# A selective-scan kernel: the products of two of four states moved to TensorE transposes, part of them to GpSimd, Softplus in one function, and the side work placed anew

## The chip, the cores and the metric

The kernel runs on one core of one Trainium2 chip. Its time is the device time of one execution in microseconds; "faster" and "slower" compare the medians of several executions. The core has five engines that each work through their own queue of instructions in program order: TensorE (PE), VectorE (DVE), ScalarE (ACT), GpSimd (POOL) and SyncE (SP, which here issues the DMAs). An instruction that waits for a semaphore holds everything behind it in its own queue, and nothing in another one.

## The reference

An image of 256 x 256 tokens with 128 channels goes through two layers, each of the form x + layer(group_norm(x)). Layer 0 is a gated attention along rows. Layer 1, in which the change lies, projects to 256 channels, applies a 3x3 depthwise convolution and SiLU, and then runs a selective scan over all 65,536 tokens in four directions (k = 0 to 3: along rows, along columns, and both backwards), with 16 states per channel:

```
delta = softplus(dt_w @ (x_proj_dt @ xs) + dt_b)          # per channel and token
h[t]  = exp(delta[t] * A) * h[t-1] + (delta[t] * xs[t]) * B[t]     # 16 states per channel
y[t]  = sum over the states of h[t] * C[t]  + D * xs[t]
```

B and C (16 values each) depend on the token, not on the channel. The four directions are summed, layer-normalised, multiplied by a gate and projected back to 128 channels.

## The kernel before

**Chunks, steps, slots.** The scan goes direction by direction (`ORDER = (2, 1, 3, 0)`) in chunks of T = 512 tokens: 128 chunks per direction, 512 in all, numbered q. A chunk has 8 steps, g = 0 to 7, one for each group of 32 channels. A tile of a step has 128 partitions: partition 32*j + c is channel c of the group with the states 4*j to 4*j+3, so `NI` = 4 states lie behind each other along the free dimension. A step handles them one after another; n = 0 to 3 counts them, and (g, n) names such a slot below: (5,3) is the last slot of step 5, and (0,0) comes after (7,3) in the next chunk. There are 4096 steps.

**What a slot does.** In each slot ScalarE computes one exponential `dA = exp(A * delta)` from `dr` (delta spread over the partitions by a DMA, through DRAM), into PSUM (`dA`) or, for one kind of state, into SBUF (`dAl`); then VectorE runs one `tensor_tensor_scan` with it. The other operand of the scan, B*delta*x, comes in two ways:

- For the first `NB` = 3 states of the four, VectorE multiplies `B_r` (B, spread over the partitions by a DMA) with `ur` (delta*x spread over the partitions by a TensorE matmul with `spread`, in PSUM), in one instruction per step, `times_B`, after the scan of slot 1.
- For the last state, ScalarE multiplies on tokens: `turn` transposes delta*x (`du`) so that tokens lie on the partitions (`tpd`, copied to `duT`); `products` multiplies it by B as a scalar per partition, 16 products of 128 x 128 for each half of the channels, into `bt`; `turn_back` transposes four blocks of it per step back into PSUM (`bl`), from which the scan reads. The slot with `bl` comes first in a step.

After the four slots GpSimd copies the last column of the step (`hst`) and multiplies the 128 x 2048 result by `C_r` (the C product). `sums` adds the states up with 16 matmuls by `gather` into `yp`, for four steps at a time: steps 0 to 3 in (5,3) and (6,0), steps 4 to 7 in (1,0) of the next chunk. `evacuate` copies `yp` to `yo`.

**Order by hand.** `tc.manual_schedule()` keeps each engine's queue in the order in which the program states the instructions. The main loop states a slot's exponential, then pieces of side work, then the scan, then (n = 1) the next step's `times_B`, and (n = 3) the next step's `bl` and the `ur` of the step after it. The side work is written as generators; each `yield` ends a piece, and one piece per slot is stated. Side work is: `prepare(q + 2)`, from (5,1) on: transposes `tps` of the tokens, copies to `xs`, the projection `pb` and its copy `bc`, the matmuls `pv`, softplus, `du`, and the loads of `B_r` and `C_r`; `turn(q + 1)` from (4,3) on; `products`, in numbers per slot given by the table `counts`; and, for a chunk that has been summed, `store` (its `tpy`, `yt`) or, in the last direction, `finish` (`ysum`, `ys`, statistics, `yn`, `tpz`, `gz`, `po`, `xo`), each from (3,0) of the next chunk on. Softplus is written out as relu(v) + log1p(exp(-|v|)), with Abs, Relu, Exp, two Identity and Ln on ScalarE and three operations on GpSimd.

**PSUM.** Eight banks: two for all side work (`tag="mm"`, in turn), one each for `bl`, `ur` and `yp`, three for `dA`. A tile with one buffer is written again only when its last reader is done.

The slots in which the pieces of `prepare` stand follow from the yields: in the kernel before, `pb` is stated in (7,0) and `bc` in (7,2); the copies of `turn` in (5,0) and (5,1).

Of the kernel before, what the change touches and what calls it, by code (L numbers as in the profile page):

```python
# [16 lines left out]
P = 128  # L17
# [49 lines left out]
def attention_and_scan_kernel(  # L67
# [568 lines left out]
    NI = 4  # L636
    NB = 3
    sw = ctx.enter_context(tc.tile_pool(name="sw", bufs=1))
# [36 lines left out]
    for q in range(4):  # L675
# [3 lines left out]
        )  # L679
    neg_one = sw.tile([P, 1], F32, name="neg_one")  # L680
    nc.vector.memset(neg_one, -1.0)
    hst = sw.tile([P, NG, NI], F32, name="hst")
# [38 lines left out]
    def prepare(q):  # L721
# [5 lines left out]
        for h in range(2):  # L727
# [6 lines left out]
            yield  # L734
        yield from until(2, 5)
        for h, tp in enumerate(tps):
# [3 lines left out]
        for h in range(2):  # L740
            nc.tensor.matmul(  # L741
                pb, xw_in[:, k, h, :], xs[:, h, :], start=(h == 0), stop=(h == 1)
            )
        yield
        yield
        bc = io.tile([R + 2 * NS, T], F32, name="bc", bufs=1)
# [3 lines left out]
        yield  # L750


        e = io.tile([P, 2, T], F32, name="e", bufs=1)
        delta = io.tile([P, 2, T], F32, name="delta", bufs=1)
        pvs = []
        for h in range(2):
            pv = sps.tile([P, T], F32, name="pv", tag="mm")
            nc.tensor.matmul(  # L758
                pv, dtw_s[:, k, h * P : (h + 1) * P], bc[:R, :], start=True, stop=True
            )  # L760
            pvs.append(pv)
        yield
        yield
        for h, pv in enumerate(pvs):
            nc.scalar.activation(e[:, h, :], pv, AF.Abs, bias=dtb_s[:, k, h : h + 1])  # L765
            nc.scalar.activation(delta[:, h, :], pv, AF.Relu, bias=dtb_s[:, k, h : h + 1])
            yield
        tp = sps.tile([P, 4, R + 2 * NS], F32, name="tpb", tag="mm")
        for b in range(4):
            nc.tensor.transpose(  # L770
                tp[:, b, :], bc[:, b * P : (b + 1) * P], ident[: R + 2 * NS, : R + 2 * NS]
            )
        nc.scalar.activation(e, e, AF.Exp, scale=-1.0)
        B_r = io.tile([P, NB, T], F32, name="B_r")
        C_r = io.tile([P, NI, T], F32, name="C_r")
        for m, t, ni in ((0, B_r, NB), (1, C_r, NI)):
            for j in range(4):
                n = m * NS + NI * j
                nc.sync.dma_start(
                    t[32 * j : 32 * j + 32],  # L780
                    bc_d[n : n + ni, :].unsqueeze(0).to_broadcast([32, ni, T]),
                )
        yield
        lg = io.tile([P, 2, T], F32, name="lg", bufs=1)
        nc.scalar.activation(lg, e, AF.Identity, bias=1.0)
        yield
        du = io.tile([P, 2, T], F32, name="du")
        nc.scalar.activation(du, lg, AF.Identity, bias=neg_one)
        B_t = io.tile([P, 4, R + 2 * NS], F32, name="B_t")
        nc.scalar.copy(B_t, tp)  # L790
        yield
        nc.gpsimd.tensor_tensor(e, e, du, ALU.subtract)  # L792
        yield
        yield
        nc.scalar.activation(lg, lg, AF.Ln)  # L795
        yield
        nc.gpsimd.tensor_tensor(lg, lg, e, ALU.add)  # L797
        yield
        nc.gpsimd.tensor_tensor(delta, delta, lg, ALU.add)  # L799
        de_d = sd.tile([DI, T], F32, name="de_d")  # L800
        nc.sync.dma_start(de_d.rearrange("(h p) t -> p h t", p=P), delta)
        yield
        nc.gpsimd.tensor_tensor(du, delta, xs, ALU.mult)  # L803
        prepared[q] = xs, de_d, du, B_r, C_r, B_t

    def turn(q):

        duT = io.tile([P, 4, DI], F32, name="duT", bufs=1)
        turned[q] = duT
        tps = []  # L810
        for w in range(2):
            tp = sps.tile([P, 2, DI], F32, name="tpd", tag="mm")
            for b in range(2):
                for h in range(2):
                    t0 = (2 * w + b) * P
                    nc.tensor.transpose(
                        tp[:, b, h * P : (h + 1) * P], prepared[q][2][:, h, t0 : t0 + P], ident
                    )
            tps.append(tp)
        yield  # L820
        for w, tp in enumerate(tps):
            nc.scalar.copy(duT[:, 2 * w : 2 * w + 2, :], tp)
            yield

    def products(q, h):


        bt = wk.tile([P, 4, 4, 4, 32], F32, name=f"bt{h}", bufs=1)
        products_of[q, h] = bt
        duT, B_t = turned[q], prepared[q][5]  # L830
        for b in range(4):
            for j in range(4):
                n = R + NI * j + NB
                nc.scalar.mul(  # L834
                    bt[:, b, :, j, :],
                    duT[:, b, h * P : (h + 1) * P].rearrange("t (g c) -> t g c", c=32),
                    B_t[:, b, n : n + 1],
                )
                yield

    def turn_back(q, g):

        bl = sps.tile([P, T], F32, name="bl", bufs=1)
        bt = products_of[q, g // 4]
        for b in range(4):
# [4 lines left out]

    def spread_delta(q, h):

        de_d = prepared[q][1]
        dr = io.tile([P, 4, T], F32, name="dr")
        for j in range(4):
            nc.sync.dma_start(
                dr[32 * j : 32 * j + 32],
                de_d[h * P : (h + 1) * P, :].rearrange("(q c) t -> c q t", c=32),
            )
        return dr  # L860
# [86 lines left out]
    def finish(q, yos):  # L947
# [39 lines left out]
        yn = io.tile([P, 4, DI], F32, name="yn", tag="yl", bufs=1)  # L987
        for j, now, then in ((0, 15, 16), (1, 16, 19), (2, 19, 20), (3, 20, 27)):
            nc.scalar.activation(
# [8 lines left out]
        for h in range(2):  # L998
# [5 lines left out]
            tps.append(tp)  # L1004
        yield from until(27, 31)
        gz = io.tile([P, 2, T], F32, name="gz", bufs=1)
        for h, tp in enumerate(tps):
# [88 lines left out]
    bls = {(0, 0): turn_back(0, 0)}
    multiplying.append(products(0, 1))
    for _ in range(4):
        piece(multiplying)


    counts = {1: [0, 0, 2, 2], 3: [2, 2, 2, 2], 5: [0, 0, 3, 3], 6: [2, 2, 2, 2], 7: [2, 2, 2, 0]}
    for s, (q, g) in enumerate(all_steps):
        k, a = steps[q]
        nxt = all_steps[s + 1] if s + 1 < len(all_steps) else None
        if g == 1:
            drs[q, 1] = spread_delta(q, 1)
        if g == 2 and q and steps[q - 1][0] != ORDER[0]:
            summed[q - 1] = load_sum(q - 1)
        if g == 2 and q + 2 < NQ:  # L1110
            load(q + 2)
        if g == 5 and q + 1 < NQ:
            drain(preparing)
            drs[q + 1, 0] = spread_delta(q + 1, 0)
        dr = drs[q, g // 4][:, g % 4, :]
        hs = bxs.pop((q, g))
        for n, i in enumerate((NB, *range(NB))):
            if i < NB:
                dA = sps.tile([P, T], F32, name="dA", bufs=3)
            else:  # L1120
# [27 lines left out]
            nc.vector.tensor_tensor_scan(  # L1148
                hs[:, i, :],
                dA,  # L1150
                hs[:, i, :] if i < NB else bls.pop((q, g)),
                0.0 if a == 0 else hst[:, g, i : i + 1],
# [12 lines left out]
        if g % 4 == 3:  # L1165
            del drs[q, g // 4]
        nc.gpsimd.tensor_copy(hst[:, g, :], hs[:, :, T - 1])  # L1167
        nc.gpsimd.tensor_tensor(hs, hs, prepared[q][4], ALU.mult)  # L1168
# [65 lines left out]
```

## Time and profile before

| what | value |
| --- | --- |
| median of 3 runs | 32186.01 us (32183.83 to 32190.26) |
| the profiled execution: its span, the only time that the page gives of it | 32185.1 us |
| busy, share of the span: VectorE, GpSimd, ScalarE, TensorE | 92%, 80%, 78%, 74% |
| first `hst` copy (end of step 0 of chunk 0) | at 5596.6 us |
| `hst` of step 0 of chunks 128, 256, 384 | at 12149.7, 18700.4, 25251.4 us |
| a chunk in the first three directions: (25251.4 - 5596.6) / 384 | 51.2 us, 6.4 per step |
| a chunk in the last direction, with `finish` (steps 3072 to 4088: 6.731 us each) | 53.85 us |
| q1, the queue of SP's DMAs: bytes | 3476.09 MB |

The layer 0 and the front of layer 1 take the first 5.5 ms. Everything after is the scan. The page gives, in its first two parts, the busy time of each engine and its busy share in 40 slices; `PEclk` is the clock granted to TensorE, in tenths of the full one. The groups list busy time, mean duration and the idle time of the engine ahead of the group's instructions, with what ended that idle time. Consecutive instructions of one engine overlap by some tens of nanoseconds, so a cost in a full queue is the distance from start to start, which the timeline gives.

### The profile page before, as it was taken

To read this page: it belongs to the slowest core of one execution; us is meant where nothing else is said; L and a number is where in the kernel's file an instruction comes from. 1 tells how busy PE (TensorE), PEld (TensorE's weight loads), DVE (VectorE), ACT (ScalarE), POOL (GpSimd) and SP (SyncE) were. 2 spreads that over 40 slices of the span, in tenths; PEclk is the share of its full clock that TensorE was granted. 3 is DMA by queue.
4 is the path that set the end of the run, shared out by engine and by line. 5 is a ranking of instruction groups with operands and counts; after the bars stand their busy time and mean duration, and the time that the engine had idled before them with its cause. 6 is when DMAs were issued, how large, how long until landed. Compare 5 with 4: busy or idle time off the path is not lost.

```text
span 32185.1 us, 380702 instructions
## 1 busy us (share of the span) xinstructions
PE 23853.4 (74%) x122902; PEld 10868.3 (34%) x122902; DVE 29575.2 (92%) x29023; ACT 25201.0 (78%) x50438; POOL 25710.4 (80%) x11291
## 2 busy tenths in 40 slices
PE   6999988666676667777777777777777777777777
PEld 3555544222222222222222232223222333333333
DVE  7666633999999999999999999999999999999999
ACT  5555522888888888888888888888888888888888
POOL 4222200999999999999999999999999999999998
PEclk9999999888888888888888888888888888888888
DMA  4001033444444444444444444444444555555554
GB/s 143 30 28 29 27 105 121 110 109 108 111 109 108 110 110 118 119 121 120 119 120 122 119 119 121 121 119 119 122 119 118 123 124 124 123 123 123 124 123 113
DMA packets 2100469, 3518.55 MB, mean 109 GB/s; under 512 B 201112, under 2 KB 1187096, under 8 KB 2022560
## 3 DMA queue, kind: packets, MB, share of 16 engines
q1 hardware_dynamic: 2093296, 3476.09, 43.3%
q8 instruction: 967, 15.84, 0.2%
q10 hardware_dynamic: 5168, 18.12, 0.1%
q14 instruction: 1038, 8.50, 0.1%
HBM read 2754.18 MB, written 739.25 MB: 109 GB/s over the span
## 4 chain that ended last, share of the span: by engine, by line
PE 32%; ACT 24%; DVE 22%; issue 12%; POOL 9%; DMA 2%; SPq 0%; ACTq 0%; POOLq 0%; DVEq 0%
DVE bx L1148 11%; PE yp L890 8%; DVE bx L875 7%; ACT dA L1122 6%; PE ur L864 6%; POOL bx L1168 5%; PE pb L741 3%; ACT bt L834 2%; PE pc L563 2%; ACT dAl L1122 2%; PE av L393 2%; PE tpy L913 2%; POOL at L370 2%; ACT e L765 2%; ACT L795 2%
## 5 line engine op out<-in xcount | busy, mean ns | idle before, releaser
L1168 POOL TENSOR_TENSOR bx<-bx,C_r 128x2048 f32<-128x2048 f32 x4096 | 18604.4, 4542 | 334.3 <-POOL hst L1167 5.8
L1148 DVE TENSOR_TENSOR_SCAN bx<-dA,hst,bx 128x512 f32<-128x512 f32 x12192 | 15074.4, 1264 | 217.2 <-ACT dA L1122 215.3
L1122 ACT ACTIVATE dA<-dr,A_s 128x512 f32<-128x512 f32 x12288 | 8329.3, 683 | 2247.5 <-DVE bx L1148 2199.6
L864 PE MATMUL ur<-du,spread 128*128 128x512 f32 x8192 | 5710.1, 787 | 4498.5 <-DVE bx L875 4378.8
L875 DVE TENSOR_TENSOR bx<-B_r,ur 128x1536 f32<-128x1536 f32 x4096 | 7075.5, 1727 | 40.1 <-DMA dr<-de_d 40.1
L834 ACT ACTIVATE bt<-duT,B_t 128x128 f32<-128x128 f32 x16384 | 5572.5, 392 | 698.7 <-PE bl L846 698.7
L1148 DVE TENSOR_TENSOR_SCAN bx<-dAl,hst,bl 128x512 f32<-128x512 f32 x4064 | 5096.6, 1254 | 24.2 <-PE bl L846 24.1
L890 PE MATMUL yp<-bx,gather 128*32 128x512 f32 x32768 | 5052.5, 771 | 7.5 <-POOL bx L1168 6.4
L846 PE MATMUL bl<-ident,bt 128*128 128x128 f32 x16384 | 2714.8, 289 | 2441.0 <-DVE bx L1148 2439.0
L846 PEld LDWEIGHTS bl<-ident,bt 128*128 128x128 f32 x16384 | 1791.0, 143 | 4323.4 <-DVE bx L1148 3240.7
L864 PEld LDWEIGHTS ur<-du,spread 128*128 128x128 f32 x8192 | 1451.2, 223 | 5027.9 <-DVE bx L875 5023.9
L370 POOL TENSOR_TENSOR at<-at,sm 128x2048 f32<-128x2048 f32 x256 | 922.2, 3603 | 2719.7 <-DVE sm L369 2550.6
L1122 ACT ACTIVATE dAl<-dr,A_s 128x512 f32<-128x512 f32 x4096 | 2919.2, 713 | 0.0
L890 PEld LDWEIGHTS yp<-bx,gather 128*32 128x32 f32 x32768 | 1165.1, 139 | 4348.3 <-issue 3834.9
L1167 POOL COPY hst<-bx 128x4 f32<-128x4 f32 x4096 | 771.4, 188 | 1615.5 <-DVE bx L1148 1588.6
L362 ACT ACTIVATE at<-at,mx 128x256 f32<-128x256 f32 x2048 | 1016.1, 498 | 472.5 <-DVE mx L358 468.1
L792 POOL TENSOR_TENSOR e<-e,du 128x1024 f32<-128x1024 f32 x512 | 1202.8, 2349 | 138.3 <-DMA C_r<-bc_d 138.3
L799 POOL TENSOR_TENSOR delta<-delta,lg 128x1024 f32<-128x1024 f32 x512 | 1209.9, 2363 | 40.1
L803 POOL TENSOR_TENSOR du<-delta,xs 128x1024 f32<-128x1024 f32 x512 | 1205.4, 2354 | 40.2
L758 PE MATMUL pv<-bc,dtw_s 8*128 8x512 f32 x2048 | 1019.6, 616 | 256.5 <-ACT bc L747 256.5
L797 POOL TENSOR_TENSOR lg<-lg,e 128x1024 f32<-128x1024 f32 x512 | 1205.0, 2354 | 0.2 <-ACT lg L795 0.2
L391 DVE COPY aT<-atp 128x512 f32<-128x512 f32 x512 | 353.6, 691 | 774.8 <-PE atp L382 771.0
(173 smaller groups left out, 31933.7 us busy)
## 6 DMA issues: line engine op xcount, KB each, us to landing
dr<-de_d SPq DMA_DIRECT2D x4096, 256.0 KB
C_r<-bc_d SPq DMA_DIRECT2D x2048, 256.0 KB
B_r<-bc_d SPq DMA_DIRECT2D x2048, 192.0 KB
de_d<-delta SPq DMA_DIRECT2D x512, 512.0 KB
xtok<-xc_d SPq DMA_DIRECT2D x256, 512.0 KB
xtok<-xc_d SPq DMA_DIRECT2D x512, 256.0 KB
yl<-y_d SPq DMA_DIRECT2D x512, 256.0 KB
y_d<-yt SPq DMA_DIRECT2D x512, 256.0 KB
```

The costliest lines, as they stand in the source:

```text
L370: nc.gpsimd.tensor_tensor(at, at, sm.unsqueeze(3).to_broadcast([P, H, 2, S]), ALU.mult,)
L797: nc.gpsimd.tensor_tensor(lg, lg, e, ALU.add)
L799: nc.gpsimd.tensor_tensor(delta, delta, lg, ALU.add)
L803: nc.gpsimd.tensor_tensor(du, delta, xs, ALU.mult)
L834: nc.scalar.mul(bt[:, b, :, j, :], duT[:, b, h * P : (h + 1) * P].rearrange("t (g c) -> t g c", c=32), B_t[:, b, n : n + 1],)
L846: nc.tensor.transpose(bl[:, b * P : (b + 1) * P], bt[:, b, g % 4].rearrange("t j c -> t (j c)"), ident)
L864: nc.tensor.matmul(ur, spread[:, g % 4].rearrange("p j c -> p (j c)"), prepared[q][2][:, g // 4, :], start=True, stop=True,)
L875: nc.vector.tensor_tensor(bx[:, :NB, :], prepared[q][3], ur.unsqueeze(1).to_broadcast([P, NB, T]), ALU.mult,)
L890: nc.tensor.matmul(yp[32 * g : 32 * g + 32, :], gather, hc[:, i, :], start=(i == 0 and steps[q][0] != ORDER[0]), stop=True, skip_group_che ...
L1122: nc.scalar.activation(dA, dr, AF.Exp, scale=A_s[:, k, g // 4, g % 4, i : i + 1])
L1148: nc.vector.tensor_tensor_scan(hs[:, i, :], dA, hs[:, i, :] if i < NB else bls.pop((q, g)), 0.0 if a == 0 else hst[:, g, i : i + 1], ALU.mult,
L1168: nc.gpsimd.tensor_tensor(hs, hs, prepared[q][4], ALU.mult)
```

## The change

- `NB` becomes 2: `times_B` covers two states, and two states of four take the way over tokens, with their own tiles `bt{h}{i}` and PSUM banks `bl0`, `bl1`. `dA` goes from three PSUM banks to two. The order of the states in a step is 2, 0, 3, 1, so that the slots 0 and 2 read `bl0` and `bl1`. `turn_back` is stated after slot 1 (`bl0`) and after slot 3 (`bl1`, ahead of `ur`).
- `products` makes 64 products per chunk, two in every slot (`PER = 2`); every fourth is a `tensor_scalar` on GpSimd (`SHARE = 4`), the others stay on ScalarE. They begin in (3,0) and (7,0).
- Softplus is one ScalarE function; the chain of Abs, Relu, Exp, Identity, Ln and the three GpSimd operations go, `du` stays on GpSimd.
- The pieces of `prepare`, `turn` and `finish` stand in other slots. By the yields `pb` is stated in (6,2), `bc` in (7,0), `pv` in (7,1), Softplus in (7,3), `du` in (0,2), the loads of `B_r` and `C_r` in (2,1); the transposes of `turn` in (1,3) and (2,0), its copies in (2,0) and (2,1). `finish` has 42 slots instead of 59.
- `dr` is loaded for two steps at a time instead of four, two steps ahead; `duT` has two buffers. Before the loop all products of chunk 0 and the whole of `prepare(1)` are made.

The diff, cut to its core:

```diff
-    NB = 3
+    NB = 2
+    SHARE = 4
...
 # prepare
-        yield from until(2, 5)
+        yield from until(2, 3)
...
-        yield
-        yield
+        yield from until(5, 7)
         bc = io.tile([R + 2 * NS, T], F32, name="bc", bufs=1)
         nc.scalar.copy(bc, pb)
...
+        yield from until(8, 10)
+        for h, pv in enumerate(pvs):
+            nc.scalar.activation(
+                delta[:, h, :], pv, AF.Softplus, bias=dtb_s[:, k, h : h + 1]
+            )
+        de_d = sd.tile([DI, T], F32, name="de_d")
+        nc.sync.dma_start(de_d.rearrange("(h p) t -> p h t", p=P), delta)
         yield
-        yield
-        for h, pv in enumerate(pvs):
-            nc.scalar.activation(e[:, h, :], pv, AF.Abs, bias=dtb_s[:, k, h : h + 1])
-            nc.scalar.activation(delta[:, h, :], pv, AF.Relu, bias=dtb_s[:, k, h : h + 1])
-            yield
         tp = sps.tile([P, 4, R + 2 * NS], F32, name="tpb", tag="mm")
...
-        nc.scalar.activation(e, e, AF.Exp, scale=-1.0)
+        yield from until(11, 13)
+        du = io.tile([P, 2, T], F32, name="du")
+        nc.gpsimd.tensor_tensor(du, delta, xs, ALU.mult)
+        B_t = io.tile([P, 4, R + 2 * NS], F32, name="B_t")
+        nc.scalar.copy(B_t, tp)
...
+        yield from until(13, 20)
         for m, t, ni in ((0, B_r, NB), (1, C_r, NI)):
...
-        nc.scalar.activation(lg, e, AF.Identity, bias=1.0)
-        nc.scalar.activation(du, lg, AF.Identity, bias=neg_one)
-        nc.gpsimd.tensor_tensor(e, e, du, ALU.subtract)
-        nc.scalar.activation(lg, lg, AF.Ln)
-        nc.gpsimd.tensor_tensor(lg, lg, e, ALU.add)
-        nc.gpsimd.tensor_tensor(delta, delta, lg, ALU.add)
...
 # turn
-            tps.append(tp)
+            yield
+            nc.scalar.copy(duT[:, 2 * w : 2 * w + 2, :], tp)
         yield
-        for w, tp in enumerate(tps):
-            nc.scalar.copy(duT[:, 2 * w : 2 * w + 2, :], tp)
-            yield
...
 # products
+        bts = [wk.tile([P, 4, 4, 4, 32], F32, name=f"bt{h}{i}", bufs=1) for i in range(NI - NB)]
+        for i, bt in enumerate(bts):
+            for b in range(4):
+                for j in range(4):
+                    n = R + NI * j + NB + i
+                    to = bt[:, b, :, j, :]
+                    of = duT[:, b, h * P : (h + 1) * P].rearrange("t (g c) -> t g c", c=32)
+                    by = B_t[:, b, n : n + 1]
+                    if SHARE and (4 * b + j) % SHARE == SHARE - 1:
+                        nc.gpsimd.tensor_scalar(to, of, by, None, ALU.mult)
+                    else:
+                        nc.scalar.mul(to, of, by)
+                    yield
...
 # finish
-        for j, now, then in ((0, 15, 16), (1, 16, 19), (2, 19, 20), (3, 20, 27)):
+        for j, now, then in ((0, 15, 16), (1, 16, 19), (2, 19, 20), (3, 20, 23)):
...
-        yield from until(27, 31)
+        yield from until(23, 25)
...
-        yield from until(55, 58)
+        yield from until(39, 41)
...
 # main loop
-        if g == 1:
-            drs[q, 1] = spread_delta(q, 1)
+        if g % 2 == 0 and s + 2 < len(all_steps):
+            drs[all_steps[s + 2]] = spread_delta(*all_steps[s + 2])
...
-        if g == 5 and q + 1 < NQ:
-            drain(preparing)
-            drs[q + 1, 0] = spread_delta(q + 1, 0)
...
-        for n, i in enumerate((NB, *range(NB))):
+        for n, i in enumerate((NB, 0, NB + 1, 1)):
             if i < NB:
-                dA = sps.tile([P, T], F32, name="dA", bufs=3)
+                dA = sps.tile([P, T], F32, name="dA", bufs=2)
...
-            if g == 4 and n == 3 and q + 1 < NQ:
+            if n == 3 and g == 1 and q + 1 < NQ:
                 turning.append(turn(q + 1))
-            if g == 5 and n == 2 and q + 1 < NQ:
+            if n == 0 and g == 3 and q + 1 < NQ:
                 multiplying.append(products(q + 1, 0))
-            if g == 7 and n == 1 and q + 1 < NQ:
+            if n == 0 and g == 7 and q + 1 < NQ:
                 multiplying.append(products(q + 1, 1))
...
-            for _ in range(counts[g][n] if g in counts else 0):
+            for _ in range(PER):
                 piece(multiplying)
...
-            if n == 3 and nxt:
-                bls[nxt] = turn_back(*nxt)
+            if n % 2 and nxt:
+                bls[(*nxt, n // 2)] = turn_back(*nxt, n // 2)
```

More of the change, by code (lines that the diff above doesn't have):

```diff
@@ L679, in attention_and_scan_kernel @@
         )
-    neg_one = sw.tile([P, 1], F32, name="neg_one")
-    nc.vector.memset(neg_one, -1.0)
     hst = sw.tile([P, NG, NI], F32, name="hst")
@@ L750, in prepare @@
         yield
-        e = io.tile([P, 2, T], F32, name="e", bufs=1)
         delta = io.tile([P, 2, T], F32, name="delta", bufs=1)
@@ L772, in prepare @@
             )
-        nc.scalar.activation(e, e, AF.Exp, scale=-1.0)
+        yield from until(11, 13)
[3 more added lines that the diff above has]
+        nc.scalar.copy(B_t, tp)
         B_r = io.tile([P, NB, T], F32, name="B_r")
         C_r = io.tile([P, NI, T], F32, name="C_r")
+        prepared[q] = xs, de_d, du, B_r, C_r, B_t
+        yield from until(13, 20)
         for m, t, ni in ((0, B_r, NB), (1, C_r, NI)):
@@ L782, in prepare @@
                 )
-        yield
-        lg = io.tile([P, 2, T], F32, name="lg", bufs=1)
-        nc.scalar.activation(lg, e, AF.Identity, bias=1.0)
-        yield
-        du = io.tile([P, 2, T], F32, name="du")
-        nc.scalar.activation(du, lg, AF.Identity, bias=neg_one)
-        B_t = io.tile([P, 4, R + 2 * NS], F32, name="B_t")
-        nc.scalar.copy(B_t, tp)
-        yield
-        nc.gpsimd.tensor_tensor(e, e, du, ALU.subtract)
-        yield
-        yield
-        nc.scalar.activation(lg, lg, AF.Ln)
-        yield
-        nc.gpsimd.tensor_tensor(lg, lg, e, ALU.add)
-        yield
-        nc.gpsimd.tensor_tensor(delta, delta, lg, ALU.add)
[L800 to L804, printed above, removed]
     def turn(q):
-        duT = io.tile([P, 4, DI], F32, name="duT", bufs=1)
+        duT = io.tile([P, 4, DI], F32, name="duT")
         turned[q] = duT
-        tps = []
         for w in range(2):
@@ L818, in turn, with turn_back @@
                     )
-            tps.append(tp)
+            yield
+            nc.scalar.copy(duT[:, 2 * w : 2 * w + 2, :], tp)
         yield
-        for w, tp in enumerate(tps):
-            nc.scalar.copy(duT[:, 2 * w : 2 * w + 2, :], tp)
-            yield
     def products(q, h):
-        bt = wk.tile([P, 4, 4, 4, 32], F32, name=f"bt{h}", bufs=1)
-        products_of[q, h] = bt
+        bts = [wk.tile([P, 4, 4, 4, 32], F32, name=f"bt{h}{i}", bufs=1) for i in range(NI - NB)]
+        products_of[q, h] = bts
         duT, B_t = turned[q], prepared[q][5]
[L831 to L844, printed above, removed]
+        for i, bt in enumerate(bts):
[10 more added lines that the diff above has]
+                    yield
+    def turn_back(q, g, i):
+        bl = sps.tile([P, T], F32, name=f"bl{i}", bufs=1)
+        bt = products_of[q, g // 4][i]
         for b in range(4):
@@ L849, in turn_back, with spread_delta @@
         return bl
-    def spread_delta(q, h):
+    def spread_delta(q, g):
         de_d = prepared[q][1]
-        dr = io.tile([P, 4, T], F32, name="dr")
+        dr = io.tile([P, 2, T], F32, name="dr")
         for j in range(4):
@@ L857, in spread_delta @@
                 dr[32 * j : 32 * j + 32],
-                de_d[h * P : (h + 1) * P, :].rearrange("(q c) t -> c q t", c=32),
+                de_d[32 * g : 32 * g + 64, :].rearrange("(q c) t -> c q t", c=32),
             )
@@ L1011, in finish @@
             yield
-        yield from until(33, 36)
+        yield from until(27, 28)
         nc.gpsimd.tensor_tensor(gz, gz, zt, ALU.mult)
-        yield from until(36, 40)
+        yield from until(28, 30)
         xr = io.tile([P, 4, D], F32, name="xr", bufs=1)
         nc.sync.dma_start(xr, x2_d[a : a + T, :].rearrange("(j p) c -> p j c", p=P))
-        yield from until(40, 55)
+        yield from until(30, 39)
         po = sps.tile([P, 4, D], F32, name="po", tag="mm")
@@ L1085, in attention_and_scan_kernel @@
     drain(preparing)
-    preparing.append(products(0, 0))
+    preparing.extend([products(0, 0), products(0, 1)])
     drain(preparing)
@@ L1091, in attention_and_scan_kernel @@
     preparing.append(prepare(1))
-    for _ in range(2 * NI + 3):
-        piece(preparing)
+    drain(preparing)
     begin_sums(0, 0)
     turning, multiplying, summing = [], [], []
[L1096 to L1102, printed above, removed]
+    bls = {(0, 0, i): turn_back(0, 0, i) for i in range(NI - NB)}
+    PER = 2
     for s, (q, g) in enumerate(all_steps):
@@ L1111, in attention_and_scan_kernel @@
             load(q + 2)
-        if g == 5 and q + 1 < NQ:
-            drain(preparing)
-            drs[q + 1, 0] = spread_delta(q + 1, 0)
-        dr = drs[q, g // 4][:, g % 4, :]
+        dr = drs[q, g - g % 2][:, g % 2, :]
         hs = bxs.pop((q, g))
-        for n, i in enumerate((NB, *range(NB))):
+        for n, i in enumerate((NB, 0, NB + 1, 1)):
             if i < NB:
-                dA = sps.tile([P, T], F32, name="dA", bufs=3)
+                dA = sps.tile([P, T], F32, name="dA", bufs=2)
             else:
@@ L1150, in attention_and_scan_kernel @@
                 dA,
-                hs[:, i, :] if i < NB else bls.pop((q, g)),
+                hs[:, i, :] if i < NB else bls.pop((q, g, i - NB)),
                 0.0 if a == 0 else hst[:, g, i : i + 1],
@@ L1164, in attention_and_scan_kernel @@
                 piece(summing)
-        if g % 4 == 3:
-            del drs[q, g // 4]
         nc.gpsimd.tensor_copy(hst[:, g, :], hs[:, :, T - 1])
@@ L1169, in attention_and_scan_kernel @@
         hcs[q, g] = hs
+        if g % 2:
+            del drs[q, g - 1]
     drain([sums(NQ - 1, 1)])
```

## The prediction

> **What bounds the kernel now.** I read the page first, for the phases, then the groups of instructions of a steady stretch, then the timeline of one chunk, then the waits. From the page:
>
> ```profile
> PE 23853.4 (74%) x122902; PEld 10868.3 (34%) x122902; DVE 29575.2 (92%) x29023; ACT 25201.0 (78%) x50438; POOL 25710.4 (80%) x11291
> DVE  7666633999999999999999999999999999999999
> PEclk9999999888888888888888888888888888888888
> ```
>
> From slice 8 on, the scan (4096 steps), VectorE is full. The groups of 12,000 to 20,000 us show what a step holds:
>
> ```profile
> L1168 POOL TENSOR_TENSOR bx<-bx,C_r 128x2048 f32<-128x2048 f32 x1251 | 5681.9, 4542 | 102.1 <-POOL hst L1167 2.0
> L875 DVE TENSOR_TENSOR bx<-B_r,ur 128x1536 f32<-128x1536 f32 x1252 | 2162.5, 1727 | 0.0
> L834 ACT ACTIVATE bt<-duT,B_t 128x128 f32<-128x128 f32 x5000 | 1699.1, 392 | 248.4 <-PE bl L846 248.4
> L1148 DVE TENSOR_TENSOR_SCAN bx<-dAl,hst,bl 128x512 f32<-128x512 f32 x1235 | 1548.4, 1254 | 4.7 <-PE bl L846 4.7
> ```
>
> The columns are busy us, mean ns, idle before. By stretch (busy us of TensorE, its loads, VectorE, ScalarE, GpSimd; then the granted clock):
>
> ```profile
> 0.00:5000.00 5000.00, 4338.66 (x30287) 2501.49 (x30290) 3099.42 (x7267) 2408.29 (x6333) 1192.96 (x395) 0.97 0.19 62
> 12000.00:20000.00 8000.00, 5697.25 (x24978) 2351.97 (x24974) 7968.93 (x6257) 6788.31 (x13133) 7332.33 (x3129) 0.83 0.49 120
> ```
>
> VectorE hardly idles; ScalarE already waits for TensorE, and why shows in the timeline of TensorE, then of ScalarE, then of VectorE, from slot (5,3) to (7,3) (start, duration):
>
> ```profile
> 15043.50 2.08 PE L864 MATMUL ur<-du,spread 128*128 128x512 f32 x2 [2.16 <-DVE bx L875]
> 15045.51 5.52 PE L890 MATMUL yp<-bx,gather 128*32 128x512 f32 x32
> 15050.95 0.66 PE L846 MATMUL bl<-ident,bt 128*128 128x128 f32 x4
> 15051.45 1.02 PE L864 MATMUL ur<-du,spread 128*128 128x512 f32 x2
> 15052.40 1.91 PE L741 MATMUL pb<-xs,xw_in 128*40 128x512 f32 x4
> ```
>
> ```profile
> 15051.65 0.69 ACT L834 ACTIVATE bt<-duT,B_t 128x128 f32<-128x128 f32 x2 [1.72 <-PE bl L846]
> 15052.25 0.67 ACT L1122 ACTIVATE dA<-dr,A_s 128x512 f32<-128x512 f32 x1
> 15052.86 0.57 ACT L1063 COPY yo<-yp 128x512 f32<-128x512 f32 x1
> 15054.35 0.58 ACT L747 COPY bc<-pb 40x512 f32<-40x512 f32 x1 [0.91 <-PE pb L741]
> 15054.83 0.69 ACT L834 ACTIVATE bt<-duT,B_t 128x128 f32<-128x128 f32 x2
> 15055.43 0.67 ACT L1122 ACTIVATE dA<-dr,A_s 128x512 f32<-128x512 f32 x1
> ```
>
> ```profile
> 15056.09 2.45 DVE L1148 TENSOR_TENSOR_SCAN bx<-dA,hst,bx 128x512 f32<-128x512 f32 x2
> ```
>
> The `sums` matmuls hold TensorE for a step's length (5.4 us); `bl`, `pb` and, on ScalarE, the copy `bc` come only after them, and ScalarE's next exponential, of slot (7,3), ends at 15056.1. VectorE wants it at 15057.3. The cover is 1.2 us: ScalarE had the exponentials up to (7,2) done before it met `bc`.
>
> **The change part by part.** Costs are from start to start.
>
> *VectorE.* Scans start 1.18 apart (15039.37, 15040.55), the multiply takes 1.65 (15041.72 to 15043.37). On two of three states it saves a third: 0.55 if all scales, 0.51 if 0.13 is fixed; I take 0.53. A step falls from 6.37 to 5.83, a chunk to 46.6; over 4096 steps 2,170 us, the whole gain.
>
> *ScalarE's sum.* Products per chunk: 48 by 0.295 (pairs of `bt` start 0.59 apart) for 32: +4.7. Abs, Relu (four by 0.57), Exp, two Identity, Ln (0.95, 0.95, 1.04, 1.08) go, two Softplus come (0.57 each, like Abs on the same operands): -5.15. ScalarE was busy 6788 / 1251 x 8 = 43.4 us per chunk, so 43 of 46.6 remain: enough on average, if nothing holds its queue. Two table loads per chunk (1283 ns each) serve Ln now. Whether Softplus needs them no row shows: 0 to 2.57 us, and I take two, Ln being the nearest row. A load at 15017.05 is followed by Ln at 15018.34, so 1.28 is all that it costs. The Trainium skill (ScalarE: Activation LUTs, "What ACT_TABLE_LOAD costs") adds a drain of 1380 ns to each switch; the rows show none, and by the page the second loss below would be 2.8 us longer and the sum some 35,000.
>
> *GpSimd.* `hst` and the C product start 4.74 apart (15042.26, 15047.00). Three of four 2.4 us operations per chunk go, 16 products come: 8 x 4.74 + 2.4 + 16X. X from below: the copies, 128x4 in 188 ns and 128x1032 in 1043, give 0.83 per element and 0.29 at 128; from above: TENSOR_SCALAR, 128x16 in 255 and 128x32 in 300, gives 2.8 and 0.57. I take 0.43, the middle, one row being of another kind and the other of another size: 47.2 us (45.0 to 49.5). In its queue `du` now stands ahead of the next `hst` and C product; those sums are due four steps later.
>
> *TensorE.* Four more transposes per step, 0.5 us. Busy time has room (71% in that stretch), order has not. The second `turn_back` waits for the step's third scan (its one buffer); behind it in TensorE's queue stand `ur`, the sums, the next `bl` and `pb`, and for these wait VectorE and ScalarE. Until now `ur` waited for the multiply only. From step 5's start: three scans and the multiply end at 4.65; 0.1, `bl` 0.5, `ur` 0.95 (2.0 in the slow case at 15043.50), sums 4.62 (5.44 here), `bl` 0.5: 11.3 (13.2). VectorE wants that `bl` at 11.66.
>
> *Where the finer placement puts ScalarE.* Three places, each priced against 5.83 us steps.
> 1. `bc` moves from (7,2) to (7,0), `pb` stays behind the sums: 11.3 + 1.9 = 13.2. Then 0.1, `bc` 0.48, two products 0.59, exponential and hand-over 0.77: 15.15 (17.05 slow). VectorE wants (7,1) at 12.8: **2.35 (4.25) lost.**
> 2. From that exponential to the one of the next (0,0) ScalarE now does: product 0.3, exp 0.61, `yo` 0.47, two products 0.59, exp 0.61, load 1.28, Softplus 1.14, product 0.3, load 1.28, exp 0.67: 7.25. VectorE has 4.65: **2.55 lost** (0 without loads). Now the Ln block sits in step 2, with three exponentials stored.
> 3. `turn` moves from (4,3) to (1,3), behind the other sums: from step 0's start, transposes end at 4.75 + 0.5 + 0.95 + 4.62 + 0.5 + 0.66 = 12.0; the copy to `duT` 0.5, products 0.59, exp 0.77 follow: 13.9, wanted at 12.8: **1.1 (3.0) lost.**
>
> Slow or full: the mean clock is 0.83; were it only full and half, half would hold a third of the time, so I add a third of 1.9 to 1 and 3: 3.0 + 2.55 + 1.75 = 7.3. The table by stretch has 0.97 where TensorE is 87% busy and 0.83 where it is 71%. The skill (TensorE: Matmul & The Clock Gate, "Part 1: The HAM clock gate") says that activity releases the throttle; by it the four transposes would bring the lower ends, 32,910 in the sum.
>
> *At nothing:* `dr` in halves: 0.5 MB two steps ahead; SP issued dr, yl and xtok, 2 MB, from 15014.0 on and yl had landed by 15026.8, so half a MB needs some 4 to 5 of 11.6 us; late, it would stop every second step. In SP's queue the `dr` for step 2 stands behind `bc_d` and `de_d`, which go out by the start of step 0 even with the losses above, two steps early; B_r and C_r, now after the `dr` for step 4, are due in the next chunk. Two `dA` banks with two `dAl` still hold four exponentials. `finish`: its copies stand in slots that have time, but two of four `yn` (0.49 each) come into (7,3) and (0,0): 1.0 per chunk, 0 if covered. Before the loop 44 more products and a drained `prepare`: 20 us (13 to 30).
>
> *Sum.* A chunk: 46.6 + 7.3 = 53.9 against 51.2, 384 times: +1,037. In the last direction 46.6 + 1.6 (bn_stats, bn_aggr: 4 x 0.33 + 4 x 0.07) + 7.3 + 1.0 = 56.5 against 53.85, 128 times: +339. With 20: +1,396 on the profiled 32,185.1 (the median is 0.9 above): **33,580 us**. All full clock: 32,910; all slow: 34,860.
>
> **The rivals.**
> *A, faster: the waits are hidden.* If the exponentials stay three ahead, VectorE (46.6) and GpSimd (47.2) bound the chunk, GpSimd the last direction (47.2 + 4.35 = 51.55): 32,185 - 384 x 4.0 - 128 x 2.3 + 20 = 30,375; with X at its ends 29,860 to 31,550. It decides if `pb` and the first transposes of `turn` are done by 10.9 instead of 13.2 and 12.0, and ScalarE meets Softplus 2.6 us ahead; the 2,439 us that TensorE waits for VectorE speak for it, the order of the sums against it.
> *B, near no change: only Softplus's block is free* (no loads, or covered): 2.55 less, 51.35 and 54.0: 32,270; at full clock 31,600. The row of Ln speaks against it.
> *C, GpSimd bounds:* needs X over 0.8 for 53.9; 0.9 would give 54.7 and 59.1, 34,200. No row is near.
>
> **How the numbers follow.** Forecast 0.70, A 0.15, B 0.12, C 0.03. Its own range is 32,910 to 34,860. To leave out no more than 2 in 10, the range drops A and the top tail and goes down through B to 31,300: 31,300 to 34,800. 0.2% is 64 us, about what a measurement of this kernel can tell from no change. Faster: A and half of B, 0.21; the same: a third of B, 0.04; slower 0.75.
>
> **What would show it.** Right: the multiply 128x1024 near 1.19 us; `bc` and `duT` idle on ScalarE waiting for `pb` and `tpd`, about 2 and over 3 us each; scans idle before `dA` by some 7 us per chunk, in steps 7, 0 and 2; two loads per chunk around Softplus; GpSimd's products 0.3 to 0.6. Wrong: scans idle under 1 us per chunk (A), no loads (B), or GpSimd never idle (C).

## The result and the profile after

The changed kernel takes 33114.44 us (median, 33108.70 to 33123.71) against 32184.92 us before: 1.029 times as long, with a 95% interval of 1.0278 to 1.0303. 33,580 us had been forecast, inside a range of 31,300 to 34,800.

From the page after (the busy times, then the busy tenths of VectorE and GpSimd in 40 slices):

```profile
PE 24928.5 (75%) x139286; PEld 13089.6 (40%) x139286; DVE 27556.1 (83%) x29022; ACT 24878.1 (75%) x55555; POOL 26866.3 (81%) x17947
DVE  7666634888888888888888888888888888888888
POOL 4222202999999999999999999999999999999999
```

VectorE has 2,019 us less to do, close to the 2,170 us that the smaller multiply was to save, and yet it is no longer full: 92% of the span became 83%. The groups of 12,000 to 20,000 us show where its idle time comes from:

```profile
L1122 DVE TENSOR_TENSOR_SCAN bx<-dAl,hst,bl 128x512 f32<-128x512 f32 x2364 | 2997.5, 1268 | 573.5 <-ACT dAl L1096 403.1 <-PE bl L827 170.4
L1122 DVE TENSOR_TENSOR_SCAN bx<-dA,hst,bx 128x512 f32<-128x512 f32 x2364 | 2980.4, 1261 | 370.0 <-ACT dA L1096 370.0
L856 DVE TENSOR_TENSOR bx<-B_r,ur 128x1024 f32<-128x1024 f32 x1198 | 1432.5, 1196 | 0.0
L817 POOL TENSOR_SCALAR bt<-duT,B_t 128x128 f32<-128x128 f32 x2397 | 1420.5, 603 | 0.0
L800 ACT COPY duT<-tpd 128x512 f32<-128x512 f32 x298 | 174.4, 585 | 681.2 <-PE tpd L796 681.2
L745 ACT COPY bc<-pb 40x512 f32<-40x512 f32 x150 | 87.2, 582 | 751.7 <-PE pb L740 751.7
```

These 8000 us hold 150 chunks. Scans idled 944 us before their exponential or their `bl`, 6.3 us a chunk; two groups of ScalarE idled before that, `bc` 5.0 us a chunk for `pb` and `duT` 4.5 us for `tpd`. The scan behind the multiply starts 1.11 us after it, 0.54 less than before. A chunk takes 53.46 us in the second and third direction (`hst` of step 0 from 12358.4 to 19201.9 us over 128 chunks), 52.9 in the first, 54.9 in the last; before it took 51.2 and 53.85. 128 x 1.7 + 256 x 2.3 + 128 x 1.1 is 950 us, the difference of the spans being 922.

The timeline of one chunk has the three places of the prediction in a row. TensorE from (5,3) on, where `ur` now comes behind the second `bl`, and the other sums, those of (1,0):

```profile
15008.10 0.75 PE L827 MATMUL bl<-ident,bt 128*128 128x128 f32 x4 [0.47 <-DVE bx L1122]
15008.68 1.02 PE L845 MATMUL ur<-du,spread 128*128 128x512 f32 x2
15009.64 3.64 PE L871 MATMUL yp<-bx,gather 128*32 128x512 f32 x32
15013.80 1.91 PE L740 MATMUL pb<-xs,xw_in 128*40 128x512 f32 x4
15032.64 5.12 PE L871 MATMUL yp<-bx,gather 128*32 128x512 f32 x32
```

ScalarE from (7,0) on: `bc` and the exponential of (7,1) behind it, the two loads around Softplus and the exponential of the next (0,0), and the copy to `duT` in (2,0):

```profile
15015.74 0.58 ACT L745 COPY bc<-pb 40x512 f32<-40x512 f32 x1 [4.48 <-PE pb L740]
15016.82 0.68 ACT L1096 ACTIVATE dA<-dr,A_s 128x512 f32<-128x512 f32 x1
15020.09 1.28 ACT L759 ACT_TABLE_LOAD   x1
15022.96 1.28 ACT L1096 ACT_TABLE_LOAD   x1
15024.25 0.72 ACT L1096 ACTIVATE dAl<-dr,A_s 128x512 f32<-128x512 f32 x1
15038.82 0.58 ACT L800 COPY duT<-tpd 128x512 f32<-128x512 f32 x1 [5.25 <-PE tpd L796]
```

VectorE, the four scans that waited in this chunk, in (7,1), (0,0), (2,0) and (2,1):

```profile
15017.53 1.28 DVE L1122 TENSOR_TENSOR_SCAN bx<-dA,hst,bx 128x512 f32<-128x512 f32 x1 [1.41 <-ACT dA L1096]
15025.01 1.28 DVE L1122 TENSOR_TENSOR_SCAN bx<-dAl,hst,bl 128x512 f32<-128x512 f32 x1 [2.72 <-ACT dAl L1096]
15038.45 1.28 DVE L1122 TENSOR_TENSOR_SCAN bx<-dAl,hst,bl 128x512 f32<-128x512 f32 x1 [1.69 <-PE bl L827]
15040.61 1.28 DVE L1122 TENSOR_TENSOR_SCAN bx<-dA,hst,bx 128x512 f32<-128x512 f32 x1 [0.88 <-ACT dA L1096]
```

1.41 + 2.72 + 1.69 + 0.88 is 6.7 us; with 46.7 of instructions that is about a chunk. One chunk is not the mean, though: in the second and third direction chunks of 52.83, 53.60 and 54.00 us follow each other in turn, and the waits differ with them. Averaged over the second direction the scan of (7,1) idles 1.65 us, that of (7,0) 0.16, that of (0,0) 2.72, that of (2,0) 1.00 and that of (2,1) 0.88: 6.4 us a chunk. One thing in the lines of the page would mislead: GpSimd is busy in 9 tenths or more of each slice of the scan, and looks like the engine that bounds.

### The profile page after: what moved, and what is told of

It is laid out like the page before. It is cut to its first block, busy times and chain, and to the rows that moved or that the text cites. A ratio compares the mean times of both kernels' runs of the same rounds, so it can differ in the third digit from the quotient of the medians.

```text
span 33106.9 us, 430509 instructions
## 1 busy us (share of the span) xinstructions
PE 24928.5 (75%) x139286; PEld 13089.6 (40%) x139286; DVE 27556.1 (83%) x29022; ACT 24878.1 (75%) x55555; POOL 26866.3 (81%) x17947
## 4 chain that ended last, share of the span: by engine, by line
PE 35%; DVE 25%; ACT 19%; POOL 12%; issue 8%; DMA 1%; SPq 0%; ACTq 0%; POOLq 0%; DVEq 0%
DVE bx L1122 15%; PE yp L871 10%; POOL bx L1140 7%; DVE bx L856 6%; ACT bt L819 5%; PE ur L845 5%; PE bl L827 4%; ACT dA L1096 3%; ACT dAl L1096 3%; PE pb L740 3%; PE pc L563 2%; PE av L393 2%; POOL bt L817 2%; POOL at L370 2%; ACT L1096 2%
## 5 line engine op out<-in xcount | busy, mean ns | idle before, releaser
L1122 DVE TENSOR_TENSOR_SCAN bx<-dAl,hst,bl 128x512 f32<-128x512 f32 x8128 | 10300.2, 1267 | 1936.5 <-ACT dAl L1096 1446.4
L827 PE MATMUL bl<-ident,bt 128*128 128x128 f32 x32768 | 6005.3, 313 | 7376.3 <-DVE bx L1122 7374.2
L1122 DVE TENSOR_TENSOR_SCAN bx<-dA,hst,bx 128x512 f32<-128x512 f32 x8128 | 10248.6, 1261 | 1231.6 <-ACT dA L1096 1231.6
L819 ACT ACTIVATE bt<-duT,B_t 128x128 f32<-128x128 f32 x24576 | 8848.1, 393 | 3.3 <-PE bl L827 3.3
L827 PEld LDWEIGHTS bl<-ident,bt 128*128 128x128 f32 x32768 | 4115.4, 158 | 10283.9 <-issue 5805.3
L1096 ACT ACTIVATE dAl<-dr,A_s 128x512 f32<-128x512 f32 x8192 | 5838.8, 713 | 210.3 <-DVE bx L1122 147.7
L1096 ACT ACTIVATE dA<-dr,A_s 128x512 f32<-128x512 f32 x8192 | 5537.8, 676 | 2.2 <-DVE bx L1122 2.2
L856 DVE TENSOR_TENSOR bx<-B_r,ur 128x1024 f32<-128x1024 f32 x4096 | 4897.7, 1196 | 31.5 <-DMA C_r<-bc_d 26.5
L817 POOL TENSOR_SCALAR bt<-duT,B_t 128x128 f32<-128x128 f32 x8192 | 4858.6, 604 | 1.9 <-ACT duT L800 1.9
L871 PE MATMUL yp<-bx,gather 128*32 128x512 f32 x32768 | 4111.7, 646 | 7.2 <-POOL bx L1140 7.2
```

Source lines behind the costliest of these rows:

```text
L817: nc.gpsimd.tensor_scalar(to, of, by, None, ALU.mult)
L819: nc.scalar.mul(to, of, by)
L827: nc.tensor.transpose(bl[:, b * P : (b + 1) * P], bt[:, b, g % 4].rearrange("t j c -> t (j c)"), ident)
L856: nc.vector.tensor_tensor(bx[:, :NB, :], prepared[q][3], ur.unsqueeze(1).to_broadcast([P, NB, T]), ALU.mult,)
L871: nc.tensor.matmul(yp[32 * g : 32 * g + 32, :], gather, hc[:, i, :], start=(i == 0 and steps[q][0] != ORDER[0]), stop=True, skip_group_che ...
L1096: nc.scalar.activation(dA, dr, AF.Exp, scale=A_s[:, k, g // 4, g % 4, i : i + 1])
```

## The experiments

Theory Q is that of the prediction: the queues of ScalarE and TensorE stand behind the sums at three places. Against it stand G (GpSimd, nearly full, bounds the chunk) and T (the added transposes load TensorE itself). A fourth one, L, came out of the first four runs. Each kernel is the changed one with the edit shown, and its ratio is to the kernel before on the same chip. Differences in us from the changed kernel are between chips, on which the kernel before took 32,181.5 to 32,192.8 us.

### One place at a time

`e1_pb_early` states `pb` ahead of the sums and leaves `bc` and the rest in their slots:

```diff
-        yield from until(2, 3)
...
-        yield from until(5, 7)
+        yield from until(5, 10)
         bc = io.tile([R + 2 * NS, T], F32, name="bc", bufs=1)
...
-            if g == 5 and n == 1 and q + 2 < NQ:
+            if g == 4 and n == 3 and q + 2 < NQ:
                 preparing.append(prepare(q + 2))
```

> Theory Q (the queues: ScalarE and TensorE stand behind the sums matmuls at three places and cost 6.7 of the 53.4 us of a chunk). prepare starts two slots earlier, in (4,3), one yield is dropped and five are added after pb, so that pb is stated in (5,3), ahead of the sums, and bc and all that follows stand where they stood. Q expects the wait of bc for pb (4.5 us) to go, the 1.4 us loss in (7,1) with it, and about 0.8 us of the 2.7 lost behind Softplus in (0,0), as ScalarE comes to it earlier: 2.2 us a chunk, 1,130 us, 31,990 us. Rival G (GpSimd bounds the chunk: 49.8 us of instructions in 53.4, over 92% busy): the products and the C product are unchanged, so within 0.3% of the kernel after. Rival T (the added transposes load TensorE itself): its work is the same, so within 0.3% too.

Measured: 32195.16 us, ratio 1.000 (0.9991 to 1.0010), 919 us less than the changed kernel, where Q had 1,130. The waits of VectorE for others in the same 8000 us (who waited for whom: us in total, times, longest):

```profile
DVE bx L1121 <- ACT dAl L1095: 292.4, 156, 2.6
DVE bx L1121 <- PE bl L826: 236.5, 157, 1.9
DVE bx L1121 <- ACT dA L1095: 137.9, 157, 0.9
```

The loss in (7,1) is gone, and the one behind Softplus has fallen from 2.7 to 1.9 us on the average (292.4 over 156), as Q said.

`e2_no_loads`:

```diff
-                delta[:, h, :], pv, AF.Softplus, bias=dtb_s[:, k, h : h + 1]
+                delta[:, h, :], pv, AF.Relu, bias=dtb_s[:, k, h : h + 1]
```

> Softplus is replaced by Relu, which changes delta and so the result, and needs no other table: two loads of 1.29 us fewer in each chunk, nothing else changes. Q: the 2.7 us lost in (0,0) fall to about 0.1; 512 times 2.6 is 1,330 us, 31,780 us, a little under the kernel before. G and T: within 0.3% of the kernel after, as neither engine has less to do.

Measured: 31998.49 us, 0.9939 (0.9924 to 0.9954), 1,116 us less, where Q had 1,330. In the same 8000 us the wait for `dAl` in (0,0) no longer occurs; the one in (7,1) became larger, 2.27 us instead of 1.65 on average in the second direction.

`e3_copy_late`:

```diff
             yield
+            if w == 0:
+                yield
+                yield
             nc.scalar.copy(duT[:, 2 * w : 2 * w + 2, :], tp)
```

> The copies of turn to duT go two slots later, from (2,0) and (2,1) to (2,2) and (2,3), with the second half of the transposes in (2,2). Q: ScalarE no longer stops 5.3 us in (2,0); the 0.9 us loss in (2,1) goes, the 1.7 us that the scan of (2,0) waits for bl stay, as TensorE's order up to there is the same: 450 us, 32,660 us. G and T: no change within 0.3%.

Measured: 32367.73 us, 1.0054 (1.0039 to 1.0069), 747 us less, more than Q's 450.

`e4_ur_first`:

```diff
-            if n % 2 and nxt:
-                bls[(*nxt, n // 2)] = turn_back(*nxt, n // 2)
             if n == 3 and s + 2 < len(all_steps):
                 urs[all_steps[s + 2]] = spread_du(*all_steps[s + 2])
+            if n % 2 and nxt:
+                bls[(*nxt, n // 2)] = turn_back(*nxt, n // 2)
```

> After slot 3 ur is stated ahead of the second bl instead of behind it, so that ur no longer waits for the third scan and the sums start some 1 to 1.9 us earlier. Q: the loss in (7,1) falls from 1.4 to about 0.5, those in (2,0) and (2,1) together from 2.6 to about 1, the one in (0,0) stays: 2 to 2.8 us a chunk, 32,000 us (31,700 to 32,200). G: no change. T: no change, TensorE's work is the same.

Measured: 32204.61 us, 1.0004 (0.9994 to 1.0013), 910 us less; Q's range was 31,700 to 32,200.

Q's sign is right four times; G and T, by which nothing should have changed by over 0.3%, are wrong four times. Q's sizes fitted in part. The length of a chunk in us, by the starts of `hst` of step 0 (the four kernels are e1 to e4 for short below):

| kernel | first direction | second and third | last |
| --- | --- | --- | --- |
| before | 51.20 | 51.18 | 53.85 |
| changed | 52.89 | 53.47 | 54.94 |
| `e1_pb_early` | 51.18 | 51.17 | 54.02 |
| `e2_no_loads` | 49.69 | 51.17 | 54.02 |
| `e3_copy_late` | 51.21 | 51.20 | 55.32 |
| `e4_ur_first` | 51.19 | 51.20 | 54.05 |

Two things in this table were not in Q. The first is GpSimd. In the last direction three of the kernels end at 54.02 to 54.05, with GpSimd (fifth busy time) busy for 98.1% of the stretch, here that of `e4_ur_first`:

```profile
26000.00:31900.00 5900.00, 4750.63 (x23773) 2518.76 (x23774) 5306.58 (x5235) 5070.88 (x11021) 5788.47 (x4147) 0.88 0.46 119
```

So they could gain only 0.9 us a chunk there, and that is most of what e1 and e2 lack. GpSimd also bounds the first direction of `e2_no_loads` (busy for 98.6% from 5700 to 11500 us). In the second direction it doesn't: of the chain of work that ended last, followed back through the profile, it holds under 0.5% in the changed kernel and in all four. In the last direction of the changed kernel it holds 48%, though `e8_share8` below, which has less work for it, takes 55.18 us there. That e3 lost 0.4 us a chunk in the last direction was not explained.

The second is 51.2 us. In the second and third direction all four kernels come to it, a gain of 2.3 us a chunk, whatever was taken away. For e1 (2.2), e2 (2.6) and e4 (2 to 2.8) that is near what Q expected; e3 was to gain 0.9. The kernel before has 51.2 too, but there VectorE's own instructions (8 steps of 6.37) explain it. The granted clock over `e4_ur_first`, by stretches that begin and end where it changes (columns: stretch, its length, busy us of TensorE, its loads, VectorE, ScalarE, GpSimd, then the clock):

```profile
14968.15:15005.70 37.55, 29.09 (x165) 14.44 (x154) 36.11 (x32) 29.69 (x68) 35.99 (x25) 1.00 0.48 125
15005.70:15019.35 13.65, 9.44 (x36) 4.11 (x38) 10.93 (x10) 13.07 (x27) 13.11 (x10) 0.51 0.29 87
15019.35:15056.90 37.55, 29.10 (x165) 14.45 (x154) 36.10 (x32) 29.70 (x68) 35.99 (x25) 1.00 0.46 125
```

The clock is full or half, nothing between; it changes on a grid of 3.413 us, whose pieces are called windows here (37.55 is 11 of them, 13.65 is 4; the kernel before has stretches of 13.65, 6.83 and 3.42); and the pattern returns every 15 windows, which is 51.2 us, the length of a chunk. In the second direction of each of the four kernels over 99% of the windows have the clock of the window 15 earlier. Which slots get the half clock differs, and with it the time of the same 32 matmuls: the sums of (1,0) take 3.64 us on average in e3, 4.36 in the changed kernel, 4.73 in e4 and 4.88 in e1. That is e3's extra gain: the scan of (2,0), whose wait Q left as it was, waits 0.28 us instead of 1.00. Theory L: TensorE's half-clock windows lie in the same slots of every chunk, the work in them is late by what they cost, and the chunk settles on a whole number of windows.

### All places, and GpSimd's share

`e6_all_places` has the edits of `e1_pb_early`, `e3_copy_late` and `e4_ur_first` together.

> The three edits of placement together: pb ahead of the sums, the copies to duT two slots later, ur ahead of the second bl. Four runs that each took away one loss of a different size (0.9 to 2.7 us a chunk expected) all came to a chunk of 51.2 us in the first three directions, which is 15 of the 3.413 us grid on which the granted clock changes. Theory Q alone (losses add up): 1.5 us left behind Softplus, 46.7 + 0.3 + 1.5 is under GpSimd's 49.8, so GpSimd bounds: 49.8 to 50.1 a chunk, 31,600 us. Theory L (the clock's grid sets the chunk: TensorE falls to half clock in the same windows of each chunk, and the wait for it holds the chunk to a whole number of windows): 51.2 again, 32,100 to 32,200 us, or 50.06 (44 windows over three chunks). Theory T: as the kernel after.

Measured: 31624.41 us, 0.9827 (0.9812 to 0.9842); 49.71 us a chunk in the first three directions. Its GpSimd in the 8000 us (fifth busy time):

```profile
12000.00:20000.00 8000.00, 6414.24 (x30907) 3123.41 (x30906) 7529.97 (x6437) 6872.35 (x15125) 7889.91 (x5310) 0.87 0.43 118
```

98.6%, where the changed kernel has 92%: GpSimd bounds, close to the 49.7 us that its instructions take from start to start (8 steps of 5.92 where nothing waits, and 2.3 for `du`). Its instructions are 62% of the chain that ended last in the second direction. Q put it at 31,600; L had a chunk of 51.2 or 50.06.

`e7_all_share8` adds one line:

```diff
-    SHARE = 4
+    SHARE = 8
```

> As the last one, with SHARE = 8: GpSimd makes 8 products of 64 instead of 16 and has 45.2 us a chunk, ScalarE 8 more by 0.295 us. Q: VectorE's 46.7 + 0.3 and some 1.5 left behind Softplus: 48.2 to 48.6 a chunk, 30,900 us. L: 47.8 (14 windows) with the last direction shorter too, 30,600 us, or 51.2 once more, 32,190 us. G (GpSimd bounds): the kernel with all placements less 4.6 us a chunk.

Measured: 30749.09 us, 0.9555 (0.9541 to 0.9569): 4.5% faster than the kernel before, with 48.2 us a chunk, which Q had and which is no whole number of windows (14.1). What is left of the waits, nearly all of it Softplus:

```profile
DVE bx L1124 <- ACT dAl L1098: 230.8, 166, 2.2
```

`e8_share8` is that line alone in the changed kernel.

> The kernel after with SHARE = 8 alone: 8 products less on GpSimd, 8 more on ScalarE, every other instruction in its place. G (GpSimd bounds the kernel after): 4.6 us a chunk less, 30,800 us. Q: GpSimd is not on the path; ScalarE gets one product more in the stretch between (7,1) and (0,0), 0.3 us: 33,100 to 33,300 us. L: the chunk stays one of 51.2 or 53.5.

Measured: 33350.04 us, 1.0366 (1.0348 to 1.0383), 236 us more than the changed kernel, a little over Q's 33,100 to 33,300. Its GpSimd is busy for 83% of the stretch, and nothing is won:

```profile
12000.00:20000.00 8000.00, 5768.59 (x28371) 2891.72 (x28369) 6974.10 (x5928) 6629.50 (x15114) 6633.11 (x3704) 0.82 0.39 108
```

L missed it, too: it had 51.2 or 53.5, and a chunk takes 53.2 in the first direction and 54.0 in the next two. So G is wrong for the changed kernel and right for `e6_all_places`: the same edit is worth -0.7% in the one and 2.8% in the other.

### How far the clock's grid holds a chunk

`e9_more_dve` and `e11_one_dve` add VectorE work to `e4_ur_first`, three times and once:

```diff
+            if n == 1 and g == 4:
+                for _ in range(3):
+                    nc.vector.bn_stats(idle, dg.rearrange("p h c -> p (h c)"))
             if n == 1 and nxt:
                 bxs[nxt] = times_B(nxt[0], urs.pop(nxt))
```

> The kernel with ur ahead of the second bl (51.2 us a chunk), and three bn_stats of 256 elements (0.33 us each, of a constant, their result unused) added on VectorE in step 4 of each chunk, where VectorE runs without a wait and ScalarE is ahead: one microsecond more in the chain from scan to scan that TensorE's order hangs on. Q alone: 1.0 us a chunk more, 510 us, 32,700 us. L: the losses shrink by what is added as long as the chunk fits in 15 windows: 51.2 us still, within 0.3% of the kernel with ur first (32,205 us).

Measured: 32555.15 us, 1.0117 (1.0102 to 1.0132), 351 us over `e4_ur_first`: between the two. A chunk takes 51.83 us, and the clock's pattern no longer returns with the chunk. L, as a rule that one chunk is a whole number of windows, is refuted by this run and by the 48.2 us above. What the traces show in its place is a pattern that returns after several chunks: 76 windows over five chunks here (they shrink from 52.94 to 52.08, 51.65, 51.43 and 51.31 us, then the next has 52.94 again), 113 over eight in `e7_all_share8`, and 47 over three in the changed kernel itself, its 52.83, 53.60 and 54.00 us.

> As the run with three added bn_stats in step 4 of each chunk, but with one: 0.33 us of VectorE's time. Three (0.98 us) made the chunk 0.63 us longer than 51.2 and ended the repetition of the clock every 15 windows. Q alone: 0.33 us a chunk, 170 us, 32,375 us. L, weakened to a plateau of some 0.35 us: 51.2 still, 32,205 us, within 0.15%.

Measured: 32204.27 us, 1.0007 (0.9998 to 1.0016), against 32204.61 without the addition, although it was done:

```profile
L1133 DVE BATCH_NORM_STATS2 idle<-dg 128x6 f32<-128x256 f32 x157 | 62.7, 399 | 0.0
```

It is paid by what the scans wait for `bl`, in the kernel with `ur` first and then in this one:

```profile
DVE bx L1122 <- PE bl L827: 34.5, 154, 0.6
```

```profile
DVE bx L1123 <- PE bl L828: 1.2, 4, 0.3
```

0.22 us of 0.33 left that wait; the rest of it went without a line of its own. So there is a plateau at 51.2, wider than 0.33 us on this side and narrower than 0.98. The clock's pattern did not stand still on it: its mean over the 8000 us is 0.90 instead of 0.87, and the sums of (1,0) take 4.41 us instead of 4.73.

### Without the plateau

> The kernel with all three placements and SHARE = 8 (48.2 us a chunk, 51.6 in the last direction, 1.4 and 2.9 of it lost around Softplus), with Relu for Softplus: delta and the result change, and the two table loads go. Q: the losses in (0,0) go entirely: 46.8 a chunk, 48.8 to 49.2 in the last direction: 384 x 1.4 + 128 x 2.6 less, 29,880 us. L (a chunk is drawn to whole windows of the clock's grid): 47.8 a chunk, 14 windows, 30,250 us. G, with GpSimd at 45.2: as Q.

`e10_all_no_loads` is `e7_all_share8` with the edit of `e2_no_loads`. Measured: 29947.19 us, 0.9307 (0.9291 to 0.9322); 46.83 us a chunk, 49.5 in the last direction, no wait of VectorE for ScalarE in the 8000 us. Q had 46.8, 48.8 to 49.2 and 29,880; L had a chunk of 47.8. Away from the plateau this loss comes off as it was priced: 48.2 - 46.83 is the 1.4 us that `e7_all_share8` lost behind Softplus.

## Why the prediction was right, and where its terms were off

**The gain** was sized right: 0.53 us a step forecast on VectorE and 0.54 measured, 5.83 us steps where nothing waits, 46.7 us of instructions in a chunk (46.6). `e10_all_no_loads`, at 46.83 us a chunk, shows it whole.

**The mechanism** was right at all three places, with the instructions named: 7.3 us a chunk were forecast to be lost, 6.3 were, over the stretch. The difference lies in place 1.

**Place 1, `bc` behind `pb` behind the sums: too large.** 2.35 to 4.25 us, 3.0 in the sum; it was 1.4 in the chunk shown, and 1.8 on average over the second direction with what (7,0) waits. The sums took 3.57 us from start to start (15009.64 to the `bl` at 15013.21), 3.67 on average, and not 4.62. Here they lay wholly in a stretch of full clock; the 4.62 us, taken for full clock, were not: from 15011.79 to 15015.21 the kernel before was at 0.50, and its sums began at 15013.03. So the lower end of the term was no bound.

**Place 2, Softplus between two loads: right.** 2.55 forecast (its terms, 7.25 less 4.65, give 2.6), 2.7 measured, and without the loads it goes (`e2_no_loads`, `e10_all_no_loads`). Two loads of 1283 ns each per chunk, as assumed from Ln's row; and no drain beside them: the load at 15022.96 starts 0.02 us behind the end of the product before it and is followed by the exponential at 15024.25, which leaves no room in this kernel for the drain of some 1380 ns that the Trainium skill states (ScalarE: Activation LUTs, "What ACT_TABLE_LOAD costs").

**Place 3, `duT` behind the other sums: right on average.** 1.75 forecast, between 1.1 and 3.0; 1.69 + 0.88 in the chunk shown, where the sums began at half clock and took 5.05; 1.00 + 0.88 on average over the second direction, with 4.36 for the sums. What was wrong is that the mean clock had been turned into a share of slow time alike for both places. It isn't: 3.67 us at the one place and 4.36 at the other, for the same 32 matmuls.

```profile
15008.55:15022.21 13.66, 12.04 (x64) 4.54 (x63) 12.25 (x11) 9.15 (x20) 12.67 (x10) 0.99 0.02 5
15022.21:15035.86 13.65, 8.79 (x32) 3.26 (x34) 10.93 (x11) 11.33 (x25) 12.95 (x8) 0.51 0.39 118
```

These are stretches of the changed kernel around the two groups of sums, with the clock behind the five busy times: 0.99 for those at 15009.64, and 0.51 for the start of those at 15032.64, at the end of a stretch in which TensorE was idle for 4.9 us of 13.65. Over the second direction of the changed kernel, cut into windows of 3.413 us, each of the 296 windows behind one in which TensorE was busy for under 30% was at half clock, and one of the 894 behind one in which it was busy for 97% or more; between these shares both occur.

**The clock as a whole.** The skill (TensorE: Matmul & The Clock Gate, "Part 1: The HAM clock gate") was weighed with the remark that more transposes would bring the lower ends. The mean clock of the stretch stayed at 0.83, with TensorE 72% busy instead of 71%: it had 2.3 us more to do in a chunk that was 2.3 us longer. The page's K of 4 or 8 in 8 does agree with the stretches above, 0.5 and 1.0.

**GpSimd's products: the size was off.** X was taken as 0.43 us, between 0.29 and 0.57; they start 0.57 apart (603 ns each), on the end that the small TENSOR_SCALAR rows gave by their 2.8 ns per element. The skill's "roughly line-rate" (GPSIMD Engine Reference, "Engine selection") is not what this operation does at 128 elements. GpSimd's chunk is thus about 49.7 and not 47.2 us. It made no difference under losses of 6 us (`e8_share8` gained nothing from less of it), and would have moved rival A: with all waits hidden the change as made could not have reached 30,375 us, as `e6_all_places` shows (31,624).

**The last direction.** 56.5 us a chunk were forecast, 54.9 measured: the `finish` copies cost what was said (0.5 more in (0,0), 0.37 in (0,1)), but place 3 there loses only 0.7 instead of 1.75 us, and place 1 2.0 instead of 3.0. The bound of GpSimd, 54.0 as `e6_all_places` shows (53.99), lies close below the 54.9. Before the loop nothing was lost; the first `hst` comes at 5588.8 us, 8 us earlier than before, where 20 us later had been forecast.

**What is not settled.** That four kernels sit at 51.2 us by the clock's grid rests on the repeating pattern, on the different times of the same sums, and on the plateau of one added operation; GpSimd, the other candidate, is not on the chain there. No run changed the clock by itself, so why a chunk is held there, and how wide such a plateau is elsewhere, was not shown.

## What to carry to other kernels

An engine's average share does not price a reordering: list what stands in front of the moved instruction in its own queue, at the moment when the work runs, and compare the time at which it comes through with the time at which the bound engine wants it. A burst on one engine (here the sums, 3.6 to 5.5 us on TensorE) is such a place, and what feeds the bound engine should not be stated shortly behind it: three edits of order and one of share turned 2.9% slower into 4.5% faster than before. And remove losses together before judging one of them, or a nearly full engine: each alone may only uncover the next bound.

## What the runs showed of the hardware

- The granted clock of TensorE switched between full and half on a grid of 3.413 us, and a loop that was bound partly by TensorE settled on 15 of these, 51.2 us: in the second and third direction five kernels with different losses (e1 to e4 and `e11_one_dve`) ran within 0.03 us of it per chunk. 0.33 us of added VectorE work cost nothing (32204.27 against 32204.61 us), while 0.98 us cost 0.63.
- 32 `yp` matmuls (16 pairs) took 3.57 us at full clock, and 5.05 and 5.44 us in the chunks shown where half-clock windows fell into them.
- A GpSimd TENSOR_SCALAR with a scalar per partition on 128 x 128 fp32 took 603 ns, the copy of 128 x 1032 only 1043 ns.
